# The FFN's scaled input made by ScalarE instead of GpSimd, in an attention and FFN block with two post-normalisations

## The chip, the cores and the metric

The kernel runs on one core of a Trainium2 chip. The metric is the device time of one execution, in microseconds (us); lower is better. A core has TensorE (matrix products and transposes, results in PSUM), VectorE, ScalarE, GpSimd and SyncE, each with an instruction queue of its own that runs in order, and 16 DMA engines. In the profile they are PE (with PEld for its weight loads), DVE, ACT, POOL and SP.

## The reference

8 sequences of 1024 tokens, 256 channels, all float32. One linear attention with 16 heads of 16 and one FFN of 1024 hidden channels with ternary weights; each is added to its input and normalised.

```python
q, k, v = x @ Wq.T + bq, x @ Wk.T + bk, x @ Wv.T + bv      # split into heads
q = softmax(q, axis=-1); k = softmax(k, axis=-2)           # over the head; over the tokens
state = einsum('bhnd,bhne->bhde', k, v)
out = einsum('bhnd,bhde->bhne', q, state)                  # heads joined
attn = ((out - mean) * rsqrt(var + EPS) * ln_g + ln_b) @ Wo.T + bo
x = layernorm(x + attn)

h = layernorm(x) * ln1_g + ln1_b
h = gelu(h @ ternary(w1).T + b1)
h = layernorm(h) * ln2_g + ln2_b
x = layernorm(x + h @ ternary(w2).T + b2)
```

## The kernel before

The 8192 tokens are worked on in 16 blocks of 512 (`len(blocks)`), two to a sequence. A block's tokens lie as four tiles of 128 tokens by 256 channels (`G = 4`), `x_of(i)[:, t, :]`.

The order of all work is written out by hand. `ORDER` is a list of short words for each step of a loop over `last + 5 = 21` steps: "early" for steps 0 to 3, "mid" for steps 4 to 15, and one list for each of the last five. `piece(what, i)` turns a word into instructions. Several blocks are under way at a time: a step projects queries and keys of one block, attends for the block before it, runs the FFN of a block further back, and finishes an older one. Small VectorE work that follows with a delay is kept in queues (`soon`, `behind`, `later`) and let out by the words beginning with `m`. Each engine runs its instructions in the order in which this program issues them; semaphores make one engine wait for another.

The words that matter here, with their lines:

- `H` (`hidden`, L696 to L686): four products of the first FFN matrix into a bank `ph`, then on ScalarE the Gelu (L702), the upper half of the product's left factor `u` (L705) and a square (L686). VectorE makes the lower half (L723, in `lower`). `A` and `B` (`product`, L770): the second FFN matrix, into four banks `pf`, two for `A`, two for `B`. After the last `A` of a block, two ScalarE copies (L783) move the first two banks to `z`; `B` then uses the same two banks. After the last `B`, two more copies.
- `p` (`apply`, L933): ScalarE normalises one tile of a block behind the attention, in place: x becomes (x - mean) / deviation, as scale times x plus a shift.
- `norm` (L597 to L632): the block's statistics on VectorE, with one power on GpSimd (L147). It also makes `rs2` (L627, L629), the inverse deviation for the FFN's own normalisation of the already normalised x.
- `en` (`enter`, L644): for each of the four tiles, `h0` = x times `rs2` (L651), the FFN's input before its gain. Then a DMA issued by GpSimd adds the FFN's output bias to x in place (L654). It must not start before `h0` has been read from x. `h0` has one buffer (two more for the last two blocks, of other tags).
- `ti` (`turn_input`, L668 to L673): TensorE transposes `h0` (L668), ScalarE and VectorE make the two halves of `hT` (L672, L673) for `H`.
- `a` (`attend`, L581): the attention's output into a bank `po`, copied by ScalarE to `o` and `y` (L586, L587). `ke` (L418): ScalarE's exponentials of the keys; they and the Gelu need different tables (ACT_TABLE_LOAD at L418 and L702). `te0`, `te2` (L430, L434): transposes of these, copied to `ek`. `x0`, `x1` (L486): products of `ek` with x into `pa`. `cr` (L518 among others): ScalarE scales the state of a sequence's first block. `qs` (L467 to L470): sum, reciprocal and product of the query softmax, the product on GpSimd.

In "mid" the word `en` stands between the first and the second of three `a` of a step:

```python
A bs m a/ph en m4 A a/w m2 m
a/w te0/tp p B te2/w be tq1/ph qe p p p B p bw qs x0 ...
```

So in the program's order, ScalarE has the `o` and `y` copies of one attention tile there, then (some steps later) the two `z` copies, two more pairs of `o` and `y`, the two `ek` copies, `qT` and the exponential of the queries. GpSimd has in its queue the DMA of L733, then L651, L654, L470 and the power of the attention's norm. `enter` for a block comes in step 3 (block 0), 4 to 15 (blocks 1 to 12), 16, 17 and 18 (blocks 13, 14, 15).

Of the kernel before, what the change touches and what calls it, by code (L numbers as in the profile page):

```python
# [11 lines left out]
AF = mybir.ActivationFunctionType  # L12
ALU = mybir.AluOpType
# [15 lines left out]
def attn_ffn_postln_kernel(  # L29
# [11 lines left out]
    nc = tc.nc  # L41
# [287 lines left out]
    def x_of(i):  # L329
        return xs[i]  # L330
# [310 lines left out]
    h0, hT, ph, u, sq, sqs, sums, sn, pf, mv, rs, sc, ms, zs = ({} for _ in range(14))  # L641
    summed = set()

    def enter(i):  # L644


        tag = {len(blocks) - 2: "q", len(blocks) - 1: "ek"}.get(i, "h0")
        h0[i] = big.tile([P, G, C], F32, tag=tag, bufs=1 + (tag == "q"), name=f"h0_{i}")
        rs2 = rs2_all[:, i * G : (i + 1) * G]
        for t in range(G):  # L650
            nc.gpsimd.tensor_scalar(  # L651
                h0[i][:, t, :], x_of(i)[:, t, :], rs2[:, t : t + 1], None, ALU.mult
            )
        nc.gpsimd.dma_start(  # L654
            x_of(i), bout.unsqueeze(1).to_broadcast([P, G, C]), accum_op=ALU.add
        )
# [327 lines left out]
    def piece(what, i):  # L984
# [76 lines left out]
        elif what == "en" and i > 2:  # L1061
            one = turn("en", NBL)
            if one:
                while one[0] not in normed:
                    more(1)
                while any(a[0] <= one[0] for a in applies):
                    apply(1)
                enter(one[0])
# [80 lines left out]
```

## Time and profile before

| | us |
|---|---|
| median of 3 runs | 660.51 |
| lowest and highest | 657.96, 661.03 |
| the profiled execution, its own time | 660.93 |
| its span, first to last instruction | 659.2 |
| L651 (h0 on GpSimd), 64 of 1.131 | 64.3 |
| L933 (normalisation on ScalarE), 64 of 0.598 | 33.5 |
| L518 (ScalarE, SBUF to SBUF, scale per row), 16 of 0.499 | 7.2 |

The mean granted TensorE clock of that execution was 0.965 of full speed; in the stretch from 340 to 412 us it was 1.00, from 570 to 659 us 0.80.

How to read the profile: the busy times of the engines overlap, and their shares are averages. The chain of waits is the work that ended last, followed back from the last instruction: at each step to what released it, or to the instruction before it on its engine. A row of a timeline gives start, length, engine, line, operation, tiles written and read, shape, how many were merged; in brackets the engine's idle time before it and what ended it. A row that merges two instructions runs from the start of the first to the end of the second; instructions of one engine overlap by a part of their length. A row of one line gives the number of its instructions and minimum, median and maximum of their durations in ns.

### The profile page before, as it was taken

What the parts mean: (1) busy time and instruction counts of PE and PEld (TensorE: products, weight loads), DVE (VectorE), ACT (ScalarE), POOL (GpSimd) and SP (SyncE); (2) the same over time, 40 slices, a digit from 0 to 9 for tenths busy, and PEclk for the clock granted to TensorE, in tenths of its full rate; (3) what the DMA queues carried; (4) which work ended last, traced back from release to release, by engine and by line L of the source; (5) the groups of instructions that cost most, each with busy time, mean ns of one, the idle gap of its engine ahead of it and who ended that gap; (6) DMA issues with size and microseconds to landing.
All of it is one profiled execution on the core that took longest, in us unless ns stands there. A gap on an engine that the chain in (4) does not pass through costs nothing.

```text
span 659.2 us, 9551 instructions
## 1 busy us (share of the span) xinstructions
PE 603.0 (91%) x3104; PEld 473.4 (72%) x3104; DVE 521.8 (79%) x1472; ACT 489.9 (74%) x923; POOL 339.5 (51%) x320
## 2 busy tenths in 40 slices
PE   5799989999999999999999999999999989887870
PEld 3467667777878687777788787878777777675760
DVE  1656678488978898888978897989898878878876
ACT  2543377879796978797896969797888878777741
POOL 1223263454466574746564664657374745775431
PEclk9889999999999999999999999999999989978885
DMA  8522233737557493858466683938484645372421
GB/s 287 216 33 33 48 77 63 157 58 159 81 129 143 92 193 61 211 87 206 74 160 135 156 149 83 206 76 200 76 181 69 132 69 118 58 128 65 96 64 64
DMA packets 51170, 77.31 MB, mean 117 GB/s; under 512 B 5265, under 2 KB 35985, under 8 KB 51121
## 3 DMA queue, kind: packets, MB, share of 16 engines
q0 software_dynamic: 26912, 49.68, 41.8%
q1 hardware_dynamic: 23936, 26.76, 12.5%
q8 instruction: 24, 0.39, 0.3%
q10 hardware_dynamic: 272, 0.26, 0.1%
q14 instruction: 26, 0.20, 0.1%
HBM read 18.24 MB, written 14.68 MB: 50 GB/s over the span
## 4 chain that ended last, share of the span: by engine, by line
PE 45%; ACT 22%; DVE 19%; issue 6%; DMA 3%; POOL 3%; SPq 1%; POOLq 0%; ACTq 0%
PE po L581 9%; PE pf L770 8%; PE pa L486 7%; PE ph L696 6%; ACT ph L702 6%; ACT sq L686 5%; PE pk L395 5%; PE pq L443 3%; DVE u L723 3%; ACT u L705 3%; DVE x L847 2%; ACT x L933 2%; PE pte L430 2%; ACT sums L686 2%; PE pth L668 2%
## 5 line engine op out<-in xcount | busy, mean ns | idle before, releaser
L770 PE MATMUL pf<-t,u 128*128 128x258 f32 x1024 | 160.9, 298 | 9.2 <-DVE u L723 6.7
L696 PE MATMUL ph<-hT,t 128*128 128x512 f32 x512 | 151.2, 428 | 8.0 <-DVE u L723 4.6
L770 PEld LDWEIGHTS pf<-t,u 128*128 128x128 f32 x1024 | 140.4, 193 | 21.8 <-DVE u L723 8.7
L723 DVE SCALAR_TENSOR_TENSOR u<-ph,gm,u 128x512 fp32r<-128x512 f32 x128 | 94.9, 747 | 50.0 <-ACT sq L686 42.8
L696 PEld LDWEIGHTS ph<-hT,t 128*128 128x128 f32 x512 | 93.5, 195 | 36.9 <-DVE u L723 13.1
L702 ACT ACTIVATE ph<-ph,bh 128x512 f32<-128x512 f32 x128 | 84.9, 663 | 24.7 <-PE ph L696 21.8
L581 PE MATMUL po<-sm,qT 128*128 128x384 f32 x256 | 91.9, 488 | 1.0 <-ACT sm L568 1.0
L705 ACT ACTIVATE u<-ph,gm 128x512 fp32r<-128x512 f32 x123 | 84.6, 688 | 4.0
L651 POOL TENSOR_SCALAR h<-x,rs_all 128x256 f32<-128x256 f32 x64 | 64.3, 1131 | 8.3 <-ACT x L933 7.3
L686 ACT ACTIVATE sq<-ph,shift 128x512 f32<-128x512 f32 x96 | 65.3, 680 | 0.1
L457 POOL TENSOR_TENSOR q<-q,qm 128x1024 f32<-128x1024 f32 x16 | 30.9, 1933 | 66.1 <-DVE qm L456 66.1
L733 POOL DMA_DIRECT2D sums<-sq x45 | 41.3, 918 | 42.9 <-issue 13.4
L486 PE MATMUL pa<-x,ek 128*128 128x256 f32 x256 | 62.0, 387 | 0.7 <-ACT ek L434 0.7
L581 PEld LDWEIGHTS po<-sm,qT 128*128 128x128 f32 x256 | 44.7, 190 | 24.7 <-ACT sm L568 4.7
L443 PE MATMUL pq<-wqkv_sb,xT 128*128 128x256 f32 x256 | 60.1, 388 | 0.0
L470 POOL TENSOR_TENSOR q<-q,rq 128x1024 f32<-128x1024 f32 x16 | 31.4, 1963 | 55.1 <-DVE rq L469 39.1
L395 PE MATMUL pk<-xT,wqkv_sb 128*128 128x512 f32 x128 | 58.0, 593 | 1.3 <-DVE q L447 1.3
L486 PEld LDWEIGHTS pa<-x,ek 128*128 128x128 f32 x256 | 48.5, 194 | 10.6 <-ACT ek L434 1.3
L147 POOL TENSOR_TENSOR ny_y<-nvy,mhalf 128x8 f32<-128x8 f32 x16 | 27.1, 1695 | 55.4 <-DVE nvy L620 55.4
L443 PEld LDWEIGHTS pq<-wqkv_sb,xT 128*128 128x128 f32 x256 | 49.5, 195 | 8.4 <-issue 1.2
L672 ACT ACTIVATE hT<-pth,gs 128x512 fp32r<-128x512 f32 x32 | 21.8, 687 | 40.3 <-PE pth L668 40.3
L147 POOL TENSOR_TENSOR ny_f<-nv_f,mhalf 128x8 f32<-128x8 f32 (+2 forms) x17 | 26.3, 1545 | 43.5 <-DVE nv_f L817 41.6
(174 smaller groups left out, 1122.4 us busy)
## 6 DMA issues: line engine op xcount, KB each, us to landing
sums<-sq POOLq DMA_DIRECT2D x45, 512.0 KB, 5.1
x<-in_x_dram SPq DMA_DIRECT2D x16, 512.0 KB, 6.9
x<-crow POOLq DMA_DIRECT2D x16, 512.0 KB, 6.0
x<-bout POOLq DMA_DIRECT2D x16, 512.0 KB, 5.9
sx_dram<-sx SPq DMA_DIRECT2D x24, 256.0 KB, 4.6
xT<-sx_dram SPq DMA_DIRECT2D x96, 64.0 KB, 3.4
out_dram<-x POOLq DMA_DIRECT2D x11, 512.0 KB, 4.5
sums<-sums POOLq DMA_DIRECT2D x13, 256.0 KB, 3.5
```

The source lines that it names most:

```text
L147: nc.gpsimd.tensor_tensor(y, v, mhalf[:, :n], ALU.pow)
L395: nc.tensor.matmul(pk, wqkv_sb[:, k, C + c * P : C + (c + 1) * P], xT[i][:, k, :], start=(k == 0), stop=(k == KC - 1),)
L443: nc.tensor.matmul(pq[:, n, :], xT[i][:, k, (t + n) * P : (t + n + 1) * P], wqkv_sb[:, k, 0:C], start=(k == 0), stop=(k == KC - 1),)
L486: nc.tensor.matmul(pa[i][:, c, :], ek[i][:, t, c * P : (c + 1) * P], x_of(i)[:, t, :], start=(t == 0), stop=(t == G - 1),)
L581: nc.tensor.matmul(po[:, c * P : c * P + P + C], qT[i][:, c, t * P : (t + 1) * P], sm[b][:, c, :], start=(c == 0), stop=(c == KC - 1), ski ...
L651: nc.gpsimd.tensor_scalar(h0[i][:, t, :], x_of(i)[:, t, :], rs2[:, t : t + 1], None, ALU.mult)
L686: nc.scalar.activation(sqs[n], ph[n], AF.Square, bias=shift)
L696: nc.tensor.matmul(ph[n], t1[:, k, j * P : (j + 1) * P], hT[i][s][:, k, :], start=(s == 0 and k == 0), stop=(s == 1 and k == KC - 1),)
L702: nc.scalar.activation(ph[n], ph[n], AF.Gelu, bias=bh[:, j : j + 1])
L705: nc.scalar.activation(u[n][:, 0, :], ph[n], AF.Copy, scale=gm[:, j : j + 1])
L723: nc.vector.scalar_tensor_tensor(u[n][:, 1, :], ph[n], gm[:, j : j + 1], u[n][:, 0, :].bitcast(F32), ALU.mult, ALU.subtract,)
L770: nc.tensor.matmul(pf[i, m][t], u[n][:, s, (2 * m + t) * P : (2 * m + t + 1) * P], t2[:, j, :], start=(j == 0 and s == 0), stop=(j == HC - ...
```

## The change

In `enter`, the four multiplications of a block are issued on ScalarE as a Copy with a scale per row, where GpSimd multiplied by the same column. Source, destination and the place in the program's order are the same. The DMA that follows stays on GpSimd's queue. On ScalarE the four instructions stand between the `y` copy of an attention tile and the `z` copies in the steps of "mid"; in step 3, 17 and 18 directly behind the block's last L933.

```diff
         for t in range(G):
-            nc.gpsimd.tensor_scalar(
-                h0[i][:, t, :], x_of(i)[:, t, :], rs2[:, t : t + 1], None, ALU.mult
+            nc.scalar.activation(
+                h0[i][:, t, :], x_of(i)[:, t, :], AF.Copy, scale=rs2[:, t : t + 1]
             )
         nc.gpsimd.dma_start(
             x_of(i), bout.unsqueeze(1).to_broadcast([P, G, C]), accum_op=ALU.add
```

In the order of instructions on each engine, ScalarE has 64 more and GpSimd 64 fewer; TensorE and VectorE have the same in the same order, and there is no further table load.

## The prediction

> **What bounds the kernel now.** I read the page first (busy shares, chain of waits), then the chain of one stage by time, then the ScalarE and TensorE timelines of that stretch. Times are in us from the start of the span; the profiled run took 660.93 us, its span 659.2.
>
> ```profile
> PE 603.0 (91%) x3104; PEld 473.4 (72%) x3104; DVE 521.8 (79%) x1472; ACT 489.9 (74%) x923; POOL 339.5 (51%) x320
> PE 45%; ACT 22%; DVE 19%; issue 6%; DMA 3%; POOL 3%; SPq 1%; POOLq 0%; ACTq 0%
> ```
>
> No engine alone is the bound: the end is set by TensorE for 45%, ScalarE for 22%, VectorE for 19%; GpSimd holds 3% of it. So the stretch that gets the moved work decides. The sixteen groups of h0 start at 90.3 to 584.5; twelve of them (blocks 1 to 12) fall once into each of the steady stages, which come every 36 us (the four normalisations of L933 start at 327.15, 363.15, 399.28, 435.28). The chain in one such stage:
>
> ```profile
> 371.79 0.68 DVE u L723
> ...
> 373.14 1.29 PE po L581 x4
> 374.43 0.48 PE pf L770 x4
> 374.91 2.58 PE po L581 x8
> 377.49 0.44 PE pte L430 x4
> 377.93 0.48 PE pf L770 x4
> ```
>
> Up to 372 the FFN half goes back and forth between ScalarE, VectorE and TensorE; from 373 to 392 the chain is TensorE alone, one matmul behind the other. What matters is how far ahead of it ScalarE is. ScalarE in the same stretch (start, length, line):
>
> ```profile
> 375.17 0.68 ACT L418 ACTIVATE ekT<-pk,nb 128x512 f32<-128x512 f32 x1
> 375.74 0.20 ACT L418 ACTIVATION_READ_ACCUMULATOR ekT<-pk,nb 128x1 f32 x1
> 375.83 0.37 ACT L586 COPY o<-po 128x256 f32<-128x256 f32 x1
> 376.08 0.39 ACT L587 COPY y<-po 128x256 f32<-128x256 f32 x1
> 376.35 0.68 ACT L783 COPY z<-pf 128x258 f32<-128x258 f32 x2
> ...
> 378.06 0.60 ACT L434 COPY ek<-pte 128x512 f32<-128x512 f32 x1
> 378.89 0.59 ACT L434 COPY ek<-pte 128x512 f32<-128x512 f32 x1 [0.22 <-PE pte L430]
> ```
>
> It has no idle time here from the end of the FFN half until 0.22 us before the second ek copy. TensorE:
>
> ```profile
> 377.33 0.60 PE L430 MATMUL pte<-ident,ekT 128*128 128x128 f32 x4
> 377.69 0.73 PE L770 MATMUL pf<-t,u 128*128 128x258 f32 x4
> ...
> 380.07 1.89 PE L486 MATMUL pa<-x,ek 128*128 128x256 f32 x8
> ```
>
> The L770 group at 377.69 opens the second half of the down projection. It needs the two banks that the z copies empty; they are empty at 376.75 and 377.03. L486 needs both ek copies, done at 379.48. ScalarE is thus ahead of TensorE by only 0.94 and 0.59 us at the two places where TensorE takes something from it.
>
> **What the change removes.** 64 GpSimd multiplications, and with them the hand-over to TensorE. In the steady stages nobody waits for them:
>
> ```profile
> 376.45 0.88 POOL L733 DMA_DIRECT2D sums<-sq  x1 [1.71 <-ACT o L586]
> 377.06 3.91 POOL L651 TENSOR_SCALAR h<-x,rs_all 128x256 f32<-128x256 f32 x4
> 381.92 1.35 POOL L654 DMA_DIRECT2D x<-bout  x1 [0.94 <-POOL h L651]
> ```
>
> h0 is complete at 380.97, and the transpose that reads it runs at 381.79 with no gap. The DMA of L654, which stays on GpSimd's queue and now waits for ScalarE there, can go out at about 378 instead of 381.92; behind it in that queue are the q product (L470, which needs VectorE's rq, done at 384.08) and the power of L147, so its earlier issue releases nobody. I count 0. What hides a collision with the transfers of xT: in the stage before, their last piece was issued at 313.1, took about 3.2 to land, and its first reader ran at 317.3; past that 1 us, each us of delay would stand before the q products.
>
> **What it adds.** Four ScalarE multiplications from SBUF to SBUF, 128x256 f32, with a scale per row, between the y copy and the z copies. The nearest row is the same function, form and scale operand:
>
> ```profile
> L518 ACT ACTIVATE a<-a,e x16: 492/496/520, 54.7 to 530.8; 128x256 f32<-128x256 f32 x16
> ```
>
> A pair of these takes 0.90 us, so the second starts 0.40 behind the first; four push what follows by 4 x 0.40 = 1.60 us. Bounds: the plain copies of L586 and L587 (PSUM source, no scale) follow each other every 0.27, 1.08 for four; L933 (scale and bias) takes 2.07 for four, a pace of 0.49, 1.97 for four. No wait comes with them in a steady stage: x was normalised some 12 us earlier (363.15 to 365.22), the h0 buffer was read in the stage before. No table load is added; the program order shows only these 64 on ScalarE.
>
> **What of it reaches the path.** Stage of 373: the first z copy ends at 376.75 + 1.60 = 378.35, L770 starts 0.05 later (about a semaphore's time) at 378.40, not 377.69: 0.71 late. The second ek copy: 1.60, less the idle times in front (0.22, and 0.05 before the third o copy) = 1.33 late, 380.81, L486 at 380.86 instead of 380.07: 0.79 late. TensorE keeps the larger, 0.8. Behind that it has no gap before the next FFN half, ScalarE waits for it there (1.42 and 1.52 before the hT copies), so nothing takes the delay back; the FFN half starts 0.8 later. Blocks 2, 4, 6, 8, 10 have this stage.
>
> The other kind of stage (410 to 417): the z copies end at 414.10 and 414.37, L770 starts at 414.74, ScalarE has no gap as far as the ek copies, which end at 416.53; L486 starts at 417.12. L770 goes to 414.10 + 1.60 + 0.05 = 415.75, 1.01 late; L486 to 416.53 + 1.60 + 0.05 = 418.18, 1.06 late. Blocks 3, 5, 7, 9, 11, and 12 by the like order: 1.05 each. Block 1 (z 124.58 to 125.25, L770 at 125.13): first bank free at 124.97 + 1.60 + 0.05 = 126.62, 1.5 late.
>
> Sum: 5 x 0.8 + 6 x 1.05 + 1.5 = 11.8 us.
>
> **The ends.** Block 0: GpSimd had started on the first tiles while ScalarE did the q exponentials; ScalarE can begin only behind the fourth L933 (91.97 + 0.49 = 92.46) and ends at 92.46 + 3 x 0.40 + 0.50 = 94.16, GpSimd at 93.94; the o and y copies now stand ahead of hT: 0.3 late. Block 14: the chain does run through GpSimd, L651 from 572.77, then L654, then the power ny_y at 577.71. But VectorE delivers that power's input only at 577.6, so not more than 0.1 comes back, while the Gelu at 574.05 and what follows it on ScalarE move by 1.60, against VectorE's L723, which was up to then 1.5 behind: about +0.15. Block 15: ScalarE has 0.70 free before 583.48, so 0.9 is left, of which VectorE's u waits but the next chain step at 585.89 hardly: 0.3. Block 13 fits into gaps: 0.1. Together 0.8 us.
>
> Total 11.8 + 0.8 = 12.6: 660.93 + 12.6 = 673.5 for a run like the profiled one. This run was 0.4 above the median of 660.51, so 673.1; I say 673. With 0.27 a piece each steady stage loses 0.52 less: 673 - 12 x 0.52 = 667; with 0.49 it loses 0.37 more: 673 + 12 x 0.37 = 677. With 1 us of doubt on each side for the ends, the forecast's own range is 665 to 679.
>
> **VectorE's relief, costed at nothing.** While GpSimd multiplies, VectorE is slower:
>
> ```profile
> 376.32 0.48 DVE L847 SCALAR_TENSOR_TENSOR x<-g2sum,ms,x 128x256 f32<-128x256 f32 x1
> 376.72 0.70 DVE L842 SCALAR_TENSOR_TENSOR x<-z,sc,x 128x256 f32<-128x256 f32 x1
> 377.45 0.87 DVE L847 SCALAR_TENSOR_TENSOR x<-g2sum,ms,x 128x256 f32<-128x256 f32 x1
> ```
>
> 0.70 and 0.87 against 0.48: about 0.6 us of VectorE a stage. The chain of this stretch has no VectorE step, so I take 0; if one sets the end, up to 0.6 x 15 = 9 us come back.
>
> The Trainium skill (GPSIMD Engine Reference, Key points) says the same of the cause: GpSimd shares SBUF interfaces with VectorE and contends with its instructions that have two SBUF inputs, and both lines have two. And in Perfetto Trace Analysis, Identifying the Most-Contended Engine, it has the bottleneck read from occupancy, TensorE's from weight loads: that makes it VectorE (79%), with ScalarE at 74% and weight loads at 72%. By this rule the change relieves the engine to optimise first, the sum would be -9 and the time 652; by the chain it is 673. I go by the chain, since these stages show TensorE without a gap.
>
> **Rivals.**
> - All of it is exposed: 64 x 0.40 = 25.6 us, 686 us (692 at L933's pace). For it: ScalarE is without a gap in the FFN half, and anything that delays it there is kept. Against it: the 0.94 and 0.59 that TensorE does not need ScalarE. Chance 0.10.
> - No change: TensorE's delay is won back where it waits for u behind the FFN half (0.40 us at 372.51), or the new instructions overlap more; 661. Against it: that wait is itself for ScalarE's and VectorE's work, which shifts along. Chance 0.08.
> - Faster, by VectorE: its 0.6 a stage in L842 and L847 (372 to 378) feeds the rq sum and hT at 382 to 387. It decides if ScalarE's push stays under the lead, that is if four pieces cost less than 0.6 us on the path, and TensorE's order then follows VectorE: 661 - 9 = 652. For it: VectorE had no gap from 373.88 to 382.29 and the page has it in 19% of the chain. Chance 0.08.
> - The forecast, a part exposed in each stage: 0.74.
>
> Range 664 to 681: the forecast's own, and the near edges of the first two rivals. A difference of 0.5% (3.3 us) is about what can be told from none: faster 0.08, same 0.08, slower 0.84.
>
> **What would show it.** L651 on ScalarE at a spacing near 0.40 ahead of the z copies; a gap of 0.7 to 1 us on TensorE before the L770 behind the first pte transposes, released by the z copy; the steady stage 36.9 to 37.1 us long instead of 36; L842 and L847 all at 0.48; no wait of the transposes for h0. I am wrong if stages stay at 36, or if TensorE's new gaps lie in the FFN half.

## The result, and the profile after

| | us |
|---|---|
| predicted | 673 (664 to 681) |
| median after, 4 runs | 670.88 (669.87 to 671.21) |
| median before on the same chip, 4 runs | 659.55 (657.96 to 661.03) |
| ratio, with its 95% interval | 1.0169 [1.0143, 1.0196] |
| profiled execution after: own time, span | 669.87, 668.2 |

The medians lie 11.3 apart; the forecast had 12.6. The page of the changed kernel, with the busy shares, the chain's shares by engine, and the matmuls of L770 (busy, mean ns of one, idle time in front and what ended most of it):

```profile
PE 604.3 (90%) x3104; PEld 471.9 (71%) x3104; DVE 511.1 (76%) x1472; ACT 512.9 (77%) x987; POOL 277.3 (41%) x256
...
PE 40%; ACT 34%; DVE 12%; issue 7%; DMA 4%; POOL 2%; SPq 1%; ACTq 0%; POOLq 0%
...
L770 PE MATMUL pf<-t,u 128*128 128x258 f32 x1024 | 161.4, 298 | 17.5 <-ACT z L783 7.6
```

The same group of L770 in the page of before:

```profile
L770 PE MATMUL pf<-t,u 128*128 128x258 f32 x1024 | 160.9, 298 | 9.2 <-DVE u L723 6.7
```

GpSimd lost 62.2 us of busy time and VectorE 10.7, ScalarE gained 23.0, and the time grew by 11.3. The chain's share of ScalarE rose from 22% to 34%. TensorE's idle time in front of L770 grew from 9.2 to 17.5, and its largest part, 7.6, is now ended by the z copies; in the waits of before no such wait is listed.

ScalarE in the stretch that answers to 375 to 379 of before (start, length, line):

```profile
382.48 0.37 ACT L586 COPY o<-po 128x256 f32<-128x256 f32 x1
382.73 0.39 ACT L587 COPY y<-po 128x256 f32<-128x256 f32 x1
382.99 1.72 ACT L651 ACTIVATE h<-x,rs_all 128x256 f32<-128x256 f32 x4
384.60 0.65 ACT L783 COPY z<-pf 128x258 f32<-128x258 f32 x2
...
386.17 1.14 ACT L434 COPY ek<-pte 128x512 f32<-128x512 f32 x2
```

From the y copy to the z copies it was 0.27 (376.08 to 376.35); it is 1.87 now. The push is 1.60. TensorE in the same stretch:

```profile
383.97 0.60 PE L430 MATMUL pte<-ident,ekT 128*128 128x128 f32 x4
...
385.03 0.78 PE L770 MATMUL pf<-t,u 128*128 128x258 f32 x4 [0.46 <-ACT z L783]
...
387.47 1.89 PE L486 MATMUL pa<-x,ek 128*128 128x256 f32 x8
```

L770 stood 0.36 behind the start of the transposes (377.33 to 377.69); now it is 1.06, with a gap that the z copy ends. L486 follows L770 by 2.44, and did so by 2.38 before: behind the one late hand-over TensorE has no second one. The chain through that stretch, piece by piece:

```profile
381.14 1.45 ACT ekT L418 x4
382.58 0.27 ACT o L586
382.85 0.27 ACT y L587
383.12 1.59 ACT h L651 x4
384.71 0.27 ACT z L783
384.99 0.04 issue
385.03 0.78 PE pf L770 x4
```

Before, it was TensorE alone from 373 on. Now it runs over ScalarE's new multiplications into the z copy and from there to TensorE.

The other kind of stage, ScalarE and TensorE together, first before, then after:

```profile
413.70 0.68 ACT L783 COPY z<-pf 128x258 f32<-128x258 f32 x2
414.74 0.73 PE L770 MATMUL pf<-t,u 128*128 128x258 f32 x4
```

```profile
421.10 1.72 ACT L651 ACTIVATE h<-x,rs_all 128x256 f32<-128x256 f32 x4
422.71 0.65 ACT L783 COPY z<-pf 128x258 f32<-128x258 f32 x2
423.14 0.78 PE L770 MATMUL pf<-t,u 128*128 128x258 f32 x4 [0.74 <-ACT z L783]
```

Its L770 is 8.40 later than before, the one at 385.03 is 7.34 later (377.69): this stage lost 1.06. The steps of all twelve, read at the first L486 of each in the two traces (us; block 1 first):

```
block   1     2     3     4     5     6     7     8     9     10    11    12
step   1.83  0.37  1.07  0.77  0.79  1.43  0.58  0.74  1.06  0.80  1.06  1.01
```

With -0.18 ahead of block 1 they make 11.33. Behind block 12 the shift between the two traces falls to 9.0, the difference of the spans, at places that hold none of the moved work: around 540 and 615 the L696 matmuls of that execution of before stand 0.43 apart and those of after 0.23 (mean granted clock from 530 to 550 and from 605 to 625 of before 0.91, in the same places of after 1.00). So the medians, 11.3 apart, are the measure, and not the two spans.

### The profile page after: what moved, and what is told of

Its sections match the earlier page's. It is cut to its first block, busy times and chain, and to the rows that moved or that the text cites. A ratio compares the mean times of both kernels' runs of the same rounds, so it can differ in the third digit from the quotient of the medians.

```text
span 668.2 us, 9549 instructions
## 1 busy us (share of the span) xinstructions
PE 604.3 (90%) x3104; PEld 471.9 (71%) x3104; DVE 511.1 (76%) x1472; ACT 512.9 (77%) x987; POOL 277.3 (41%) x256
## 3 DMA queue, kind: packets, MB, share of 16 engines
q1 hardware_dynamic: 23936, 26.76, 12.6%
## 4 chain that ended last, share of the span: by engine, by line
PE 40%; ACT 34%; DVE 12%; issue 7%; DMA 4%; POOL 2%; SPq 1%; ACTq 0%; POOLq 0%
PE pf L770 7%; ACT sq L686 7%; ACT ph L702 7%; PE pa L486 6%; PE ph L696 6%; PE pq L443 5%; PE pk L395 5%; PE po L581 4%; ACT h L651 3%; ACT u L705 3%; ACT ekT L418 3%; ACT x L933 3%; ACT L418 2%; DVE u L723 2%; PE pth L668 2%
## 5 line engine op out<-in xcount | busy, mean ns | idle before, releaser
L770 PE MATMUL pf<-t,u 128*128 128x258 f32 x1024 | 161.4, 298 | 17.5 <-ACT z L783 7.6
L770 PEld LDWEIGHTS pf<-t,u 128*128 128x128 f32 x1024 | 139.8, 192 | 33.2 <-ACT z L783 10.5
L696 PE MATMUL ph<-hT,t 128*128 128x512 f32 x512 | 148.8, 423 | 7.1 <-DVE u L723 4.0
L723 DVE SCALAR_TENSOR_TENSOR u<-ph,gm,u 128x512 fp32r<-128x512 f32 x128 | 95.1, 747 | 47.8 <-ACT sq L686 40.4
L696 PEld LDWEIGHTS ph<-hT,t 128*128 128x128 f32 x512 | 92.5, 192 | 35.4 <-DVE u L723 11.4
L486 PE MATMUL pa<-x,ek 128*128 128x256 f32 x256 | 61.6, 385 | 0.7 <-ACT ek L434 0.7
L443 PE MATMUL pq<-wqkv_sb,xT 128*128 128x256 f32 x256 | 60.1, 387 | 0.4 <-DMA xT<-sx_dram 0.4
L486 PEld LDWEIGHTS pa<-x,ek 128*128 128x128 f32 x256 | 48.2, 193 | 10.3 <-ACT ek L434 1.1
L443 PEld LDWEIGHTS pq<-wqkv_sb,xT 128*128 128x128 f32 x256 | 49.2, 194 | 8.9 <-issue 1.0
L654 POOL DMA_DIRECT2D x<-bout x16 | 21.1, 1320 | 50.4 <-ACT z L783 25.3
```

The costliest lines, as they stand in the source:

```text
L443: nc.tensor.matmul(pq[:, n, :], xT[i][:, k, (t + n) * P : (t + n + 1) * P], wqkv_sb[:, k, 0:C], start=(k == 0), stop=(k == KC - 1),)
L486: nc.tensor.matmul(pa[i][:, c, :], ek[i][:, t, c * P : (c + 1) * P], x_of(i)[:, t, :], start=(t == 0), stop=(t == G - 1),)
L696: nc.tensor.matmul(ph[n], t1[:, k, j * P : (j + 1) * P], hT[i][s][:, k, :], start=(s == 0 and k == 0), stop=(s == 1 and k == KC - 1),)
L723: nc.vector.scalar_tensor_tensor(u[n][:, 1, :], ph[n], gm[:, j : j + 1], u[n][:, 0, :].bitcast(F32), ALU.mult, ALU.subtract,)
L770: nc.tensor.matmul(pf[i, m][t], u[n][:, s, (2 * m + t) * P : (2 * m + t + 1) * P], t2[:, j, :], start=(j == 0 and s == 0), stop=(j == HC - ...
```

## The experiments

Two readings stood against each other. By "lead", each stage loses only what of ScalarE's push (the time by which the added work delays what stands behind it) exceeds the lead (the time for which a result lies ready before TensorE takes it) at the hand-overs. By "share", the time follows how much work ScalarE has, wherever it stands. Ratios are against before on the same chip, with 95% intervals; the medians of before were 659.12 for the first four, 658.99 for the next four, 659.62 for the last three.

**1. The multiplications behind the ek copies.** The word `en` is moved in "mid", the same 64 instructions stay on ScalarE.

```diff
-            m8 A st2/w tq0/tp A m1 A H A H A st3/w A ke p m2 tx1/w A bs m a/ph en m4 A a/w m2 m
-            a/w te0/tp p B te2/w be tq1/ph qe p p p B B p bw qs x0 m3 ti1/ph p m4 m2 m1 m4 a/tp
+            m8 A st2/w tq0/tp A m1 A H A H A st3/w A ke p m2 tx1/w A bs m a/ph m4 A a/w m2 m
+            a/w te0/tp p B te2/w en be tq1/ph qe p p p B B p bw qs x0 m3 ti1/ph p m4 m2 m1 m4 a/tp
```

> The four ScalarE multiplications of a steady stage stand behind the second ek copy, ahead of the qT copy, instead of ahead of the z copies. Theory of the lead (what is lost in a stage is the push of 1.60 us less the time that ScalarE is ahead of TensorE at the next hand-over): the z and ek copies come as early as in the kernel before, the next hand-over is hT behind 1.42 us of ScalarE's idle time, so a stage loses 0.1 to 0.3 us; 660 to 664 us. Theory of the share (the added 25.6 us of ScalarE time cost a fixed 0.44 of themselves wherever they stand): 671 as with the change.

Measured: 662.0, 1.0038 [1.0018, 1.0058]. Three quarters of the loss are gone (2.9 left of 11.3) with ScalarE as busy as in the changed kernel (513.7). Share is refuted. ScalarE in this kernel:

```profile
380.34 0.59 ACT L434 COPY ek<-pte 128x512 f32<-128x512 f32 x1 [0.22 <-PE pte L430]
380.83 1.71 ACT L651 ACTIVATE h<-x,rs_all 128x256 f32<-128x256 f32 x4
...
383.00 1.06 ACT L462 ACTIVATE q<-q 128x1024 f32<-128x1024 f32 x1
383.96 0.67 ACT L672 ACTIVATE hT<-pth,gs 128x512 fp32r<-128x512 f32 x1
```

The 1.42 us that ScalarE had free ahead of hT swallow the push. About 0.4 in every second stage remains; in the trace the q exponential is late there, behind it VectorE's sum rq, and then VectorE's part of u. Experiment 10 bears on that.

**2. Half of them.**

```diff
         for t in range(G):
-            nc.scalar.activation(
-                h0[i][:, t, :], x_of(i)[:, t, :], AF.Copy, scale=rs2[:, t : t + 1]
-            )
+            if t < 2:
+                nc.scalar.activation(
+                    h0[i][:, t, :], x_of(i)[:, t, :], AF.Copy, scale=rs2[:, t : t + 1]
+                )
+            else:
+                nc.gpsimd.tensor_scalar(
+                    h0[i][:, t, :], x_of(i)[:, t, :], rs2[:, t : t + 1], None, ALU.mult
+                )
```

> Two of a block's four tiles are multiplied by ScalarE at the change's place, two by GpSimd. Theory of the lead: the push is 0.80 us, the leads of 0.59 to 0.94 us take it in five stages, six lose 0.25, block 1 loses 0.7: about 2.2 us, 662. Theory of the share: half of the change's 11.3 us, 665.

Measured: 662.11, 1.0054 [1.0028, 1.008]. Half of the push costs 3.0 by the medians and 3.6 by the ratio, a quarter to a third of the loss, not half of it: a push of 0.8 stays under the lead in one kind of stage (steps of 0.0 in blocks 2 and 4) and passes it a little in the other (0.24 to 0.29 in blocks 3, 11 and 12; 0.25 expected). Between them, in blocks 6 to 10, the steps of this execution scatter from -0.2 to 2.7, as TensorE waits for other things. The longest of these waits:

```profile
286.01 1.32 PE L443 MATMUL pq<-wqkv_sb,xT 128*128 128x256 f32 x5 [2.41 <-DMA xT<-sx_dram]
```

It is for one of the transfers of xT with which, by the prediction, L654's earlier DMA could collide. They come up again below.

**3. Each multiplication twice**, into the same tile.

```diff
         for t in range(G):
-            nc.scalar.activation(
-                h0[i][:, t, :], x_of(i)[:, t, :], AF.Copy, scale=rs2[:, t : t + 1]
-            )
+            for _ in range(2):
+                nc.scalar.activation(
+                    h0[i][:, t, :], x_of(i)[:, t, :], AF.Copy, scale=rs2[:, t : t + 1]
+                )
```

> ScalarE does the four multiplications of a block twice, at the change's place. Theory of the lead: the lead is used up, every further us is lost: 12 stages x 1.6 = 19 us more than with the change, and up to 4 more at the ends; 690 to 694. Theory of the share: another 11.3 us, 682.

Measured: 718.3, 1.0909 [1.0854, 1.0963]. Both theories missed, by 24 and more. The kernel's own timeline of ScalarE and TensorE shows two causes:

```profile
371.85 0.95 PE L771 MATMUL pf<-t,u 128*128 128x258 f32 x4 [2.92 <-ACT z L784]
372.60 1.05 PE L430 MATMUL pte<-ident,ekT 128*128 128x128 f32 x4
...
407.24 3.89 ACT L652 ACTIVATE h<-x,rs_all 128x256 f32<-128x256 f32 x8
...
411.45 0.78 PE L771 MATMUL pf<-t,u 128*128 128x258 f32 x4 [2.63 <-ACT z L784]
412.07 0.60 PE L430 MATMUL pte<-ident,ekT 128*128 128x128 f32 x4
```

At 407 eight multiplications take 3.89, a push of 3.80 where 3.2 was taken (two into one tile do not stand 0.40 apart). And behind the gap of 2.92 the same transposes take 1.05 instead of the 0.60 behind that of 2.63; the granted TensorE clock is 0.55 from 373 to 376 and 1.00 from 411 to 414. What each of the two causes costs was not taken apart. So this run does not test the theories; experiment 5 does it without either.

**4. Both engines do it.** From before: GpSimd makes h0, and ScalarE makes the same products into one spare tile that nobody reads. It should leave VectorE as slow as before and so price its relief.

```diff
+        aside = big.tile([P, C], F32, tag="o", bufs=4, name=f"aside_{i}")
         for t in range(G):
             nc.gpsimd.tensor_scalar(
                 h0[i][:, t, :], x_of(i)[:, t, :], rs2[:, t : t + 1], None, ALU.mult
             )
+            nc.scalar.activation(aside, x_of(i)[:, t, :], AF.Copy, scale=rs2[:, t : t + 1])
```

> GpSimd makes h0 as before, and ScalarE does the same four multiplications at the change's place into a tile that nobody reads: the change's added ScalarE time without the removal from GpSimd. If VectorE's relief from GpSimd gives nothing back on the path (as forecast): the same as with the change, 670 to 672. If the relief of up to 9 us is worth something and hides a part of the loss: slower than the change by that much, up to 680.

Measured: 675.96, 1.026 [1.0229, 1.0291]: 16.8 above before where the change alone has 11.3, which looks like a relief worth 5.5. But its row in ScalarE's timeline

```profile
385.98 2.15 ACT L655 ACTIVATE aside<-x,rs_all 128x256 f32<-128x256 f32 x4
```

is 0.43 longer than the four of the changed kernel (1.72): the four write one tile, and the next stands 0.55 behind the one ahead. Twelve stages of 0.43 make 5.2, so this run can't tell a relief from the longer push. Experiment 6 keeps the push at 1.60.

**5. Six instead of four**, with tiles 0 and 1 done again at the end, so that no two neighbours write one tile.

```diff
-        for t in range(G):
+        for t in (0, 1, 2, 3, 0, 1):
             nc.scalar.activation(
```

> Six multiplications at the change's place instead of four (tiles 0 and 1 once more behind tile 3), so that no instruction waits for the one just before it and TensorE's gap stays under 2 us. Theory of the lead: each of the two more costs 0.40 us in each of 12 steady stages, 9.6 us more than with the change's 670.9, and up to 2 at the ends: 680 to 683. Theory of the share: half of 11.3 more, 676 to 677.

Measured: 682.8, 1.0362 [1.0329, 1.0395], the value of lead. The kernel is 23.8 above before: two more multiplications cost 12.5 more, where four cost 11.3. Past the lead every 0.40 counts whole: 2 x 0.40 x 12 = 9.6 were worked out for the twelve stages, and by the traces they lost 10.0 more than with the change; the gaps in front of L770 are 1.23 and 1.54 now (0.46 and 0.74). The rest, some 2.5, lies outside them or in the scatter of the medians; its cause is open.

**6. Both engines, three spare tiles**, in the buffers of `aT` and `sT`; on top of the changed kernel.

```diff
+        two = big.tile([P, KC, C], F32, tag="aT", name=f"two_{i}")
+        one = big.tile([P, KC, P], F32, tag="sT", name=f"one_{i}")
+        aside = [two[:, 0, :], two[:, 1, :], one.rearrange("p k c -> p (k c)")]
         for t in range(G):
-            nc.scalar.activation(
-                h0[i][:, t, :], x_of(i)[:, t, :], AF.Copy, scale=rs2[:, t : t + 1]
-            )
+            nc.gpsimd.tensor_scalar(
+                h0[i][:, t, :], x_of(i)[:, t, :], rs2[:, t : t + 1], None, ALU.mult
+            )
+            nc.scalar.activation(aside[t % 3], x_of(i)[:, t, :], AF.Copy, scale=rs2[:, t : t + 1])
```

> GpSimd makes h0 as before, ScalarE does the four multiplications at the change's place into three spare tiles in turn, so that they follow each other every 0.40 us as with the change (in the earlier run all four wrote one tile and took 2.06 us). If VectorE's relief is worth nothing on the path: 670 to 672, as with the change. If it is worth something: 675 and more, as in the earlier run.

Measured: 669.87, 1.0164 [1.0133, 1.0194], against 1.0169 [1.0143, 1.0196] of the changed kernel. VectorE and TensorE in it:

```profile
381.26 0.70 DVE L846 SCALAR_TENSOR_TENSOR x<-z,sc,x 128x256 f32<-128x256 f32 x1
382.00 0.88 DVE L851 SCALAR_TENSOR_TENSOR x<-g2sum,ms,x 128x256 f32<-128x256 f32 x1
...
382.93 0.79 PE L774 MATMUL pf<-t,u 128*128 128x258 f32 x4 [0.46 <-ACT z L787]
```

VectorE is again slowed down (0.70 and 0.88; busy 520.0), TensorE's gap is the 0.46 of the changed kernel, and the time is the same. So VectorE's relief, and GpSimd's work, are worth nothing here that can be told from the scatter of the medians.

**7. Behind the z copies, ahead of the ek copies.** This tells the two hand-overs of the prediction apart.

```diff
-            m8 A st2/w tq0/tp A m1 A H A H A st3/w A ke p m2 tx1/w A bs m a/ph en m4 A a/w m2 m
+            m8 A st2/w tq0/tp A m1 A H A H A st3/w A ke p m2 tx1/w A bs m a/ph m4 A en a/w m2 m
```

> The change with the four multiplications directly behind the z copies. Theory of the lead, with both hand-overs: the z copies are on time, but the ek copies are late by 1.60 less 0.59 and ScalarE's small gaps, 0.8 and 1.06 us a stage: 669 to 672, as with the change. If the z copies alone made the loss: 660 to 663.

Measured: 663.6, 1.0072 [1.0048, 1.0096]. The prediction's price for the ek hand-over (0.79 and 1.06 a stage) would have left the loss nearly whole. What is left of the loss shows at L486, in the second kind of stage as a gap:

```profile
417.82 1.14 ACT L434 COPY ek<-pte 128x512 f32<-128x512 f32 x2
...
418.53 1.78 PE L486 MATMUL pa<-x,ek 128*128 128x256 f32 x7 [0.32 <-ACT ek L434]
```

The gap is 0.32, and TensorE goes on at 418.53 while the second copy ends at 418.96. So L486 starts on the first ek copy alone; the second is needed by its third product. In the first kind of stage the profile marks no gap, but the same hand-over decides there too:

```profile
379.69 1.19 PE L770 MATMUL pf<-t,u 128*128 128x258 f32 x8
380.16 1.15 ACT L434 COPY ek<-pte 128x512 f32<-128x512 f32 x2
380.88 2.00 PE L486 MATMUL pa<-x,ek 128*128 128x256 f32 x8
```

L486 starts 1.19 behind this L770, where it was 1.03 in the kernel before (379.04 to 380.07), and 0.06 behind the end of the first ek copy (380.82). In this trace the stages of the first kind lose about 0.3 each, the undisturbed ones of the second kind 0.5 to 0.6, and block 1 loses 1.25, with a gap of 0.80 in front of its L486. So with the z copies on time 6.7 of the 11.3 are gone, and the late ek copies account for about what is left, 4.6.

**8. As 1, and ScalarE relieved elsewhere**: L933 of blocks 1 to 12 goes to GpSimd.

```diff
-                nc.scalar.activation(x_t, x_t, AF.Identity, bias=sh, scale=rs)
+                if 0 < i < len(blocks) - 3:
+                    nc.gpsimd.tensor_scalar(x_t, x_t, rs, sh, ALU.mult, ALU.add)
+                else:
+                    nc.scalar.activation(x_t, x_t, AF.Identity, bias=sh, scale=rs)
```

> As the first experiment (ScalarE's multiplications behind the ek copies), and GpSimd takes the normalisation of L933 for blocks 1 to 12 in exchange: ScalarE loses 2 us a stage in the FFN half, where it has no gap. TensorE is idle for only 0.2 to 0.6 us of a 36 us stage, so at most 5 us come of it: 656 to 662. If GpSimd's queue comes late with the DMAs of L733 or L654 for it: 665 and more.

Measured: 660.73, 1.0021 [1.0005, 1.0037], 1.7 above before where 1 had 2.9. The intervals of the two overlap, so this is no proven gain over 1, and it is not faster than before.

**9. The opposite of the change**: before, with the edit of 8 alone.

> The opposite exchange on the kernel before: h0 stays on GpSimd, and GpSimd also takes the normalisation of L933 for blocks 1 to 12; ScalarE loses 2 us a stage where it has no gap and gets nothing. Theory of the lead: it counts only as far as TensorE waits there, 0.2 to 0.6 us a stage: 655 to 659. If every us of ScalarE counts by a share of 0.44: 12 x 2.0 x 0.44 = 10 us less, 649.

Measured: 659.31, 0.9997 [0.9982, 1.0012]. ScalarE's busy time falls from 489.9 to 466.8, and nothing comes of it: just outside the 655 to 659 of lead, and far from the 649 of share. But the relief was not clean. TensorE in one of its stages:

```profile
368.56 1.20 PE L696 MATMUL ph<-hT,t 128*128 128x512 f32 x4 [0.60 <-DVE u L723]
```

In the kernel before the same group started at 367.99 without a gap. VectorE's part of u comes 0.58 later here (367.76 against 367.18), since small VectorE instructions in front of it take longer while GpSimd does the moved normalisation (365.42 to 367.82; L407 at 367.25 takes 0.59, before 0.16); VectorE's busy time is 528.4 instead of 521.8. So 23 us less on ScalarE bring nothing when they are bought this way; what they would bring alone stays open.

**10. Behind the q exponential too.**

```diff
-            a/w te0/tp p B te2/w be tq1/ph qe p p p B B p bw qs x0 m3 ti1/ph p m4 m2 m1 m4 a/tp
+            a/w te0/tp p B te2/w be qe en tq1/ph p p p B B p bw qs x0 m3 ti1/ph p m4 m2 m1 m4 a/tp
```

(`en` is gone from between the two `a` as in 1.)

> The change with ScalarE's four multiplications behind the ek copies and the queries' exponential, ahead of the qT copy, which no one needs before the next step. Theory of the lead: the exponential is no longer late for VectorE's rq sum (in the first experiment that cost 0.4 us in every second stage), h0 is in time for its transposes to within 0.1 us: 658 to 661. If the rest of the first experiment's loss had another cause: 662 as there.

Measured: 660.49, 1.0013 [0.9998, 1.0027]. With the exponential ahead of the multiplications the remainder is 0.9, which can't be told from no change; the interval overlaps a little with that of 1, so the gain over 1 is likely and not proven. ScalarE in it:

```profile
381.28 1.05 ACT L462 ACTIVATE q<-q 128x1024 f32<-128x1024 f32 x1
382.23 1.69 ACT L651 ACTIVATE h<-x,rs_all 128x256 f32<-128x256 f32 x4
```

The four multiplications cost ScalarE the same 1.6 here. All that TensorE shows of it in this stage is that the transposes of h0, at 383.60, take 0.70 instead of 0.60. In two other stages it waits for a piece of xT (0.36 and 0.33 in front of L443).

**11. Edits 10 and 8 together.**

> The same order, and GpSimd takes the normalisation of L933 for blocks 1 to 12 in exchange. The two effects add: 655 to 659. If GpSimd's queue comes late with the DMAs behind the normalisation: 661 and more.

Measured: 660.18, 1.0008 [0.9992, 1.0024]. A gain over before was expected, and there is none; as in 9, TensorE waits longer for VectorE's u (0.64 in a stage of the first kind). No version tried beats the kernel before.

## Why the prediction was right, step by step

**The place.** It was named: the L770 that opens the second half of the down projection, released by the z copy. The waits of the changed kernel show it (7.6 us in 11 cases for the matmuls), and moving the work behind the z copies takes 6.7 of 11.3 away (7).

**The size of the push.** 4 x 0.40 = 1.60 from the pairs of L518; measured 1.60 by the y-to-z distance. The new row has 516 ns for one (L518 had 496), at the same spacing. The ends of the bound, 0.27 and 0.49, were not needed.

**What of it reaches the path.** First kind of stage: 0.8 predicted, 4.11 / 5 = 0.82 measured, but this mean hides two stages that differ. Block 2 lost only 0.37: TensorE waits there 0.83 for VectorE's u before and after the change, so the z copy leads L770 by 1.34 (159.26 to 160.60 in before) and not by 0.94, and push less lead gives 0.3. The prediction counted this stage with the others. Block 6 lost 1.43, of which 0.40 is a wait for a transfer (below). The other three lost 0.77 to 0.80; the z hand-over alone had been worked out as 0.71.

Second kind: 1.05 predicted, 5.57 / 6 = 0.93 measured, with four of the six at 1.01 to 1.07, where z alone gave 1.01. The two low ones, blocks 5 and 7, come from the execution of before: from L486 to L486 these stages took 37.32 and 37.55 there and the others of this kind 37.05, with a wait for VectorE's u in front of L696 (0.20 and 0.43) that the traces of experiments 1, 6 and 8 do not have in these blocks. After the change blocks 3, 5, 7, 9 and 11 all have 38.11 to 38.13.

Block 1: 1.5 predicted, 1.83 measured. Of this, 0.29 was there before its z copies (the shift between the traces goes from -0.18 to 0.11 at its first L430); that is block 0's end, and block 1's own part is 1.54.

Sum: 11.8 predicted, 11.5 measured. That the sums come so near is partly luck: block 2 and the two long stages of before make the measured one smaller, block 6's transfer and block 0's end make it larger.

**The step that was wrong: the ek hand-over.** The prediction let L486 wait for both ek copies and took the larger of the two delays. Experiment 7 shows that its first products wait only for the first copy; that copy leads L486 by 1.40 and 1.16 in the two kinds of stage of before, where the prediction took 0.59. With only this hand-over late, a stage lost about 0.3 and 0.5 to 0.6, where 0.79 and 1.06 were predicted. It did little harm because in the changed kernel the z copies delay L770 first and L486 follows without a wait, and because the two predicted delays lay within 0.1 of each other: by z alone the sum is 5 x 0.71 + 6 x 1.01 + 1.5 = 11.1 instead of 11.8. For a kernel with only the ek hand-over, the same step is wrong by more than half of the loss: 669 to 672 expected in experiment 7, 663.6 measured.

**Ends.** 0.8 was predicted. In the traces block 0's transposes are 0.48 late, and 0.3 of it is left in front of block 1 (0.3 predicted); it is already in block 1's 1.83. Block 13 shows nothing, block 14 +0.17 at L723 (0.15 predicted), block 15 about 0.1 (0.3). That is some 0.6 by the rows, and nothing by the medians (11.3 against 11.5 for the twelve stages). The whole overshoot, 12.6 against 11.3, is inside the interval of the ratio (9.4 to 12.9 us), so it can't be shared out more finely.

**The signs that were named.** The spacing of 0.40 is there, and the stages of the two kinds, 35.82 and 38.12, have the mean 36.97, as forecast (36.9 to 37.1). The gap in front of L770 was to be 0.7 to 1 us; the profile marks 0.46 to 0.49 and 0.73 to 0.75 (none above 0.15 in block 2). It counts from the end of the four transposes ahead, and these take 0.60, while L770 used to start 0.36 behind their start. From start to start L770 is later by 0.70 and 0.98.

**VectorE's relief, costed at nothing.** L842 and L847 are now nearly all at 0.48 (7 of 128 above 0.52, 38 before), and VectorE's busy time is 10.7 lower: both as predicted. Experiment 6 gives the slowdown back, and the time stays within the scatter. The rival with 652 is refuted, and with it the reading of occupancy that put VectorE first; in these stages TensorE's order decides.

**L654's earlier DMA, costed at nothing.** Nearly right. It goes out at 385.65 where it would have been at 389.3 (381.92 + 7.4), and in one stage it collides with the pieces of xT, as the 1 us of cover allowed for. First TensorE in block 6's stage of the changed kernel, then the transfers of 268 to 296 (KB each, us from issue to landing):

```profile
287.92 3.26 PE L443 MATMUL pq<-wqkv_sb,xT 128*128 128x256 f32 x14 [0.40 <-DMA xT<-sx_dram]
```

```profile
x<-bout POOLq DMA_DIRECT2D x1, 512.0 KB, 9.8
...
sx_dram<-sx SPq DMA_DIRECT2D x1, 256.0 KB, 7.6
```

In the same stretch of before the two took 8.0 and 5.6. It costs 0.40 once in this execution, 2.41 once in that of experiment 2, and 0.36 and 0.33 in that of experiment 10; the execution of experiment 5, with the same hand-over to L654, shows no such wait. That it is the earlier issue was not tried by an edit of its own.

**The other rivals.** All exposed (686) is refuted by the result, and by 1 and 2; no change (661) by the result: the wait for u in which the delay was to be won back, 0.40 at 372.51, is still there (0.41 at 379.15).

## What to carry to other kernels

Where one engine runs without a gap, price work on another one at the first place where the first takes something from it: push minus lead, once per stage, and nothing below the lead. Read the lead in every stage: here it was 0.16 in block 1, 1.34 in block 2, and 0.64 to 0.94 in the others. The work that an engine has in sum says little: the same 64 instructions cost 11.3 us ahead of the z copies, 4.6 between the z and the ek copies, 2.9 behind the ek copies, and behind the q exponential 0.9, which can't be told from nothing. When a consumer needs several pieces, look which piece its first instruction needs before the last one is taken for the release.

## What the runs showed of the hardware

- ScalarE's instructions into different tiles stand 0.40 apart (four in 1.72), into one tile 0.52 to 0.57 (four in 2.15 in experiment 4; eight in 3.89 in experiment 3, pairs into one tile). An experiment that doubles a write to the same tile measures more than the doubled work.
- TensorE ran at half pace for some us around a gap a little under 3 us. In experiment 3, five of six gaps of 2.90 to 2.92 were followed by matmuls of 128 columns of 414 to 421 ns (four times at once, once from the third matmul on), and three of four gaps of 2.63 to 2.66 by such of 269 to 274 ns; behind the fourth (329.94) the pace halved some 1.4 us later. The granted clock was 0.50 to 0.56 in these stretches and 1.00 in the others. The Trainium skill (TensorE: Matmul & The Clock Gate, Part 1: The HAM clock gate) tells of a halved clock after an idle window of about 3.4 us, counted freely; the gaps here were already enough at 2.9, once at 2.65. Around the changed kernel's gaps of 0.4 to 1.2 the granted clock stayed at 1.00.
